# One quad more fetched row by row, from two queues, and the second last quad folded into one table

## The chip, the cores and the metric

The kernel runs on one core of a Trainium2 chip. Its engines are named as in the profile: PE (TensorE), DVE (VectorE), ACT (ScalarE), POOL (GpSimd) and SP (SyncE, which here only issues DMAs and loads registers). The metric is the device time of one execution in microseconds (us); the median of several runs is compared.

## The reference

A layer of graph attention. 12,500 nodes with 128 features, 200,000 edges sorted by their target `dst`, four heads of 32:

```python
h = relu(layernorm(x)) @ W_node.T                  # per node, 4 heads x 32
att = a . [h[src], h[dst], edge @ W_edge.T]        # per edge and head
att = where(att > 0, att, 0.2 * att)
m = maximum(segment_max(att, dst), 0)
ex = exp(att - m[dst])
denom = segment_sum(ex, dst) + (E - deg) * exp(-m)
out = x + segment_sum(ex / denom[dst] * h[src], dst)
```

## The kernel before

**Tiling.** The edges are cut into 392 groups of 511 edges and one entry that carries a running sum in. A group is 4 chunks of 128 edges, four groups are a *quad* (98 quads, 0 to 97), and one to four quads are a *super* whose softmax is done at once (the last supers have 2, 2 and 1 quads). A node's row in the DRAM tensor `table` has 137 floats (548 bytes): its 4 x 33 values, a count and 4 source logits.

**Rows by source.** The rows `h[src]` of a quad are 16 chunks of 128 rows. POOL fetches a chunk with one indirect DMA (`gather`, line 185), into one of eight places of `ga_all` (quad q into place q % 8). Quad 84 (`SINGLE`) is an exception: `gather` skips it, and SP fetches its 2,048 rows with one DMA each. `single_rows` (line 677) does eight rows at each step of `sums`, from quad 11 on: 16 steps a chunk, 256 steps, four steps a quad, so it ends with quad 74. Rows go into `GA[84]`, a part of `db_all` that is free after quad 9. The row numbers of a chunk are fetched by SP into one of two rows of 128 words (`fetch_places`), multiplied to byte offsets by DVE (`scale_places`) and loaded into registers 16 at a time (line 692). Two semaphores count the landings, and ACT waits for them in `add_sources` (line 790).

**Order of the work.** The program is written out by hand in Python generators that are stepped in turn; each engine works in the order in which its instructions are issued. In a stretch of the main loop (lines 1677 to 1711) `all_logits(q)` makes the attention logits of a quad with PE, DVE and ACT (it also asks for the gather of quad q + 2), `softmax(s)` does a super, and `sums(q)` weighs the gathered rows (`weighed`, line 1109), marks which edge goes to which node (`mark`) and adds up on PE (line 1186). `add_sources(q)` is where ACT copies the source logits out of the gathered rows (`U`, line 798): it waits there for the quad's gather. `all_logits(q)` calls it for quad q - 1 in the same stretch in which `sums(q - 5)` runs. `SP` loads features, offsets, weights and inputs two quads ahead (`issue`, line 606).

**Windows.** Quads 0 to 74 sum several groups into one window of nodes. From quad 75 on each group has a window of its own of 80 nodes: row 0 of its accumulator is the running sum of a node that goes on in the next group, so each window takes the row of the one before it in (`carried_in`, line 986, on ACT or DVE, then a matmul on line 983), and `copied_out` moves the accumulator to `pt`. A quad is then divided and its four windows are stored one by one (`divide`, `divide_by_gpsimd`); SP waits before each store to `out` until the one before it has landed.

**The end.** `finale` (line 1618) is the order of the last two supers, quads 95 and 96 and quad 97, written out. The last quad (`first_fold` = 97) is done by `folded` (line 1287): its four windows are moved into one table of 3 x 112 nodes by matmuls with 0/1 matrices (`SHIFT`, made by `shifts` on DVE four quads earlier), divided once and stored by one DMA (`finish`). Quad 96 goes through `sums` as others do, in two halves. `values_load` on line 1652 puts the flag that decides on the slow path (line 1714) into a register of every engine.

Of the kernel before, what the change touches and what calls it, by code (L numbers as in the profile page):

```python
# [14 lines left out]
OP = mybir.AluOpType  # L15
# [30 lines left out]
FOLDS, PARTS, FINE = 1, 3, 3  # L46
# [3 lines left out]
SINGLE, SINGLES_FROM, AT_A_STEP = 84, 11, 8  # L50
# [20 lines left out]
def kernel(  # L71
# [86 lines left out]
    first_fold = nq - FOLDS  # L158
    g_fold = quads[first_fold][0]
    assert class_of(first_fold) == (1, NARROW)  # L160
# [9 lines left out]
    single_came = [tc.alloc_semaphore(f"single{k}") for k in range(2)]  # L170
    landings = {}

    def gather(q, rows, width, lo, hi):

        if q == SINGLE:
            return
# [38 lines left out]
    assert [m for _, m in supers[-FINE:]] == [2, 2, FOLDS] and quads[-1][1] == QG  # L215
# [332 lines left out]
    with tc.tile_pool(name="work", bufs=2) as work, \  # L548
# [74 lines left out]
        def fetch_inputs(q):  # L623
# [3 lines left out]
            if q >= first_fold:  # L627
                at = ROWS[q] = windows(base_row, 4 * D, w, 1)
                due["inputs"].append((as_bytes(xw[1:1 + WIDE, 0:PARTS, :]), nodes_at(x, at[0])))
                return  # L630
# [12 lines left out]
        def fetch_rows(s):  # L643
            g0, m = groups(s)
            dr = DR[s] = turned.tile([SBG * H, NE + 2], I32, name="dr", bufs=2)
            if finer(s) > 1:
# [8 lines left out]
        n_own = QG * J * ROW  # L655
        GA[SINGLE] = own[:, QG * GE // 2:QG * GE // 2 + n_own].bitcast(F32).rearrange(
            "p (g j r) -> p g j r", g=QG, j=J)
        places = [own[0:1, QG * GE // 2 + n_own + k * P:QG * GE // 2 + n_own + (k + 1) * P]
                  for k in range(2)]
        single = {"step": 0, "landings": 0}  # L660
        steps = -(-P // AT_A_STEP)

        def fetch_places(n):

            if n >= QG * J:
                return
            g, j = quads[SINGLE][0] + n // J, n % J
# [3 lines left out]
        def scale_places(n):  # L671

            if n < QG * J:
# [3 lines left out]
        def single_rows():  # L677
# [5 lines left out]
            if n >= QG * J:  # L683
# [6 lines left out]
            lo = at * AT_A_STEP  # L690
            if at % 2 == 0:
                single["values"] = nc.values_load_multi_w_load_instructions(
                    places[n % 2][:, lo:lo + 2 * AT_A_STEP], engines=[mybir.EngineType.SP],
                    min_val=0, max_val=(NP - 1) * 4 * ROW,
                    skip_runtime_bounds_check_because="a node's row")[1]
            for p in range(lo, lo + AT_A_STEP):
                came = nc.sync.dma_start(
                    as_bytes(GA[SINGLE][p:p + 1, n // J, n % J, :]),
                    rows_at(table, single["values"][p - at // 2 * 2 * AT_A_STEP], 4 * ROW, 1))
                came.then_inc(single_came[2 * n // (QG * J)], 16)  # L700
# [1236 lines left out]
```

## Time and profile before

| | |
|---|---|
| median of 3 runs | 1971.07 us (1969.68 to 1973.94) |
| the profiled execution | 1973.07 us, span of its instructions 1971.2 us |
| busy: POOL, DVE, PE, PE weight load, ACT | 1477.5, 1193.8, 1134.6, 771.6, 318.1 us |
| mean granted TensorE clock | 0.739 |
| share of the DMA engines that the queues took: POOL's, SP's, ACT's | 24.5%, 21.0%, 0.4% |

A span is cut by time (windows), by instruction group (line, engine, operation), by wait (who waited for whom: total us, times, longest) or followed back from its last instruction (the chain). In a timeline a row is: start, duration, engine, line, operation, out<-in; the bracket holds the idle time before it and who ended that. "SPq" and "ACTq" are the queues of an engine that issue DMAs and load registers, not its arithmetic. In a view of one line, durations are in ns as minimum/median/maximum, then the first and the last start.

### The profile page before, as it was taken

How to read it: one execution, taken by the hardware profiler on the slowest of the kernel's cores; microseconds unless marked ns; L12 is line 12 of the kernel's file. 1: busy time of each engine (PE TensorE's matmuls, PEld its weight loads, DVE VectorE, ACT ScalarE, POOL GpSimd, SP SyncE). 2: the span in 40 equal slices, each digit the busy share in tenths (PEclk: the TensorE clock that was granted, in tenths of full speed). 3: DMA queues.
4: the chain of work that ended last, by engine and by line, in shares of the span. 5: the costliest groups of instructions: out<-in, count | busy, mean ns of one | idle time of the engine just before them, and what ended most of it. 6: DMA issues, size and time to landing. Idle time of an engine off the chain costs nothing.

```text
span 1971.2 us, 23138 instructions
## 1 busy us (share of the span) xinstructions
PE 1134.6 (58%) x5116; PEld 771.6 (39%) x5116; DVE 1193.8 (61%) x2631; ACT 318.1 (16%) x1077; POOL 1477.5 (75%) x1569
## 2 busy tenths in 40 slices
PE   6666676454555554646556555555464755555565
PEld 4544444333333342434334333344242433334344
DVE  8676887365464663746546546466374663767576
ACT  6664111001010010100000101001011011212122
POOL 7777777777777777777777777777777777777775
PEclk9788788676776766767767677777676766877678
DMA  7754754434444444444444444444444444544442
GB/s 257 209 134 100 177 135 107 106 93 107 103 106 107 102 113 102 117 101 118 104 119 103 114 108 113 110 112 110 113 109 99 105 122 109 128 114 116 98 107 56
DMA packets 171399, 229.87 MB, mean 117 GB/s; under 512 B 62636, under 2 KB 104542, under 8 KB 171255
## 3 DMA queue, kind: packets, MB, share of 16 engines
q0 software_dynamic: 49600, 108.49, 24.5%
q1 hardware_dynamic: 119952, 117.28, 21.0%
q10 hardware_dynamic: 1702, 2.59, 0.4%
q14 instruction: 104, 0.84, 0.1%
q8 instruction: 41, 0.67, 0.1%
HBM read 210.75 MB, written 17.43 MB: 116 GB/s over the span
## 4 chain that ended last, share of the span: by engine, by line
POOL 29%; DVE 27%; PE 15%; issue 13%; DMA 9%; ACT 5%; SPq 2%; ACTq 0%; POOLq 0%; DVEq 0%
POOL ga L185 29%; DMA ga<-table,srci 6%; PE acc L1186 6%; DVE at L717 4%; PE t_ps L855 2%; PE lg L747 2%; DVE ga L1112 2%; DVE t_ps L869 1%; DVE t_ps L868 1%; DVE t_ps L935 1%; DVE t_ps L932 1%; PE lg L750 1%; DVE pt L1019 1%; DVE hot L1095 1%; PE ex_ps L950 1%
## 5 line engine op out<-in xcount | busy, mean ns | idle before, releaser
L185 POOL DMA_INDIRECT ga<-table,srci x1478 | 1399.8, 947 | 451.8 <-issue 408.9
L1186 PE MATMUL acc<-ga,hot 128*113 128x137 f32 (+1 forms) x2904 | 536.3, 344 | 83.9 <-DVE hot L1095 43.4
L1186 PEld LDWEIGHTS acc<-ga,hot 128*113 128x113 f32 (+1 forms) x2904 | 476.5, 214 | 183.8 <-issue 78.9
L1019 DVE SCALAR_TENSOR_TENSOR pt<-pt,spare,acc 1x133 f32<-1x133 f32 x113 | 38.3, 339 | 484.4 <-ACT den_of L1013 483.0
L750 PE MATMUL lg<-at,pw 112*96 112x512 bf16 (+2 forms) x392 | 155.8, 434 | 266.6 <-DVE at L717 239.4
L717 DVE TENSOR_TENSOR at<-const_ps,db 112x1024 bf16<-112x1024 f32 (+1 forms) x176 | 212.9, 1211 | 43.4 <-DMA db<-offset 41.6
L747 PE MATMUL lg<-ea,by_pair 128*96 128x512 f32 (+1 forms) x392 | 229.5, 671 | 7.1 <-ACT tg L760 7.1
L1153 DVE TENSOR_TENSOR ga<-ga,ex_ps 128x1056 f32<-128x1056 f32 x145 | 179.7, 1240 | 0.0
L855 PE MATMUL t_ps<-ident,U 128*64 128x128 f32 (+2 forms) x210 | 46.4, 391 | 216.6 <-ACT U L798 216.6
L798 ACT COPY U<-ga 128x64 f32<-128x64 f32 x97 | 28.7, 297 | 786.7 <-DMA ga<-table,srci 786.7
L1155 DVE TENSOR_TENSOR hot<-const_ps,slot 128x896 f32<-128x896 f32 (+1 forms) x147 | 144.2, 981 | 0.0
L855 PEld LDWEIGHTS t_ps<-ident,U 128*64 128x64 f32 (+2 forms) x210 | 36.5, 198 | 242.8 <-ACT U L798 239.5
L950 PE MATMUL ex_ps<-ident,stack 128*128 128x128 f32 x105 | 28.5, 423 | 173.0 <-DVE stack L942 162.3
L750 PEld LDWEIGHTS <-pw 112*96 112x96 bf16 (+2 forms) x392 | 54.3, 139 | 103.3 <-issue 97.8
L1038 PEld LDWEIGHTS acc<-pt,spare 1*2 1x2 f32 x226 | 14.0, 86 | 204.2 <-issue 195.4
L950 PEld LDWEIGHTS ex_ps<-ident,stack 128*128 128x128 f32 x105 | 18.5, 214 | 186.9 <-ACT stack L940 186.9
L1112 DVE TENSOR_TENSOR ga<-ga,ex_ps 128x528 f32<-128x528 f32 x92 | 63.6, 693 | 37.3 <-ACT xs L956 37.2
L185 POOL DMA_INDIRECT ga<-in_x_dram,srci x72 | 68.5, 951 | 23.3 <-issue 18.9
L760 ACT COPY tg<-lg 96x512 f32<-96x512 f32 (+1 forms) x51 | 29.5, 579 | 297.4 <-PE lg L750 297.4
L776 PE MATMUL t_ps<-tg,of_head 96*64 96x512 f32 (+3 forms) x96 | 72.4, 848 | 0.0
L776 PEld LDWEIGHTS t_ps<-tg,of_head 96*64 96x64 f32 (+3 forms) x96 | 11.9, 171 | 146.0 <-issue 144.0
L747 PEld LDWEIGHTS lg<-ea,by_pair 128*96 128x96 f32 (+1 forms) x392 | 63.4, 187 | 13.2 <-ACT tg L760 8.6
(222 smaller groups left out, 1306.8 us busy)
## 6 DMA issues: line engine op xcount, KB each, us to landing
ea<-in_edge_t_dram SPq DMA_DIRECT2D x196, 256.0 KB
db<-table SPq DMA_DIRECT2D x2048, 0.5 KB
ga<-table,srci POOLq DMA_INDIRECT x1478, 3.7
db<-offset SPq DMA_DIRECT2D x53, 256.0 KB
db<-in_dst_dram SPq DMA_DIRECT2D x20, 320.0 KB
db<-offset SPq DMA_DIRECT2D x35, 160.0 KB
table<-row SPq DMA_DIRECT2D x9, 616.5 KB
xt<-in_x_dram SPq DMA_DIRECT2D x9, 576.0 KB
```

The source lines that it names most:

```text
L185: came = nc.gpsimd.indirect_dma_start(out=ga[:, i, j, 0:width], out_offset=None, in_=rows, in_offset=bass.IndirectOffsetOnAxis(ap=srci[:, ...
L717: nc.vector.tensor_tensor(AT[q][:span, i:i + n, :].rearrange("p g e -> p (g e)"), part_ps[:span].to_broadcast([span, n * GE]), DB[q][:span ...
L747: nc.tensor.matmul(lg, by_pair[:, begin:begin + n], ea[:, i // 2, :], start=half == 0 and i == 0, stop=False, skip_group_check=True)
L750: nc.tensor.matmul(lg, PW[q][:span, begin:begin + n], at[:span, i, :], start=False, stop=full and i == quads[q][1] - 1, skip_group_check=True)
L776: nc.tensor.matmul(TP[s][:groups(s)[1] * H], of_head[supers[s][1], p][:n], tg[:n], start=p == 0, stop=False, skip_group_check=True)
L855: nc.tensor.matmul(t_ps[:R, j * P:(j + 1) * P], u[:, j, :R], ident, start=False, stop=j == C - 1, skip_group_check=True)
L950: nc.tensor.transpose(turned_ps[:, j, :], stack[:, j * P:(j + 1) * P], ident)
L1019: nc.vector.scalar_tensor_tensor(to, row(w + at), passing[:, w + at:w + at + 1], own, op0=OP.mult, op1=OP.add)
L1112: engine.tensor_tensor(val, val, weight.unsqueeze(3).to_broadcast([P, J, H, HW]), op=OP.mult)
L1153: nc.vector.tensor_tensor(val, val, weight.unsqueeze(3).to_broadcast([P, TWO * J, H, HW]), op=OP.mult)
L1155: nc.vector.tensor_tensor(hot[:, i:i + TWO, :, 1:1 + span].rearrange("p g j c -> p (g j) c"), lane_ps[:, 0:span].unsqueeze(1).to_broadcast ...
L1186: nc.tensor.matmul(acc, hot[:, i, j, 0:1 + span], ga[:, i, j, :], start=new and j == J - 1 and not second, stop=k > 1 and i % k == k - 1 a ...
```

## The change

Two things, and a third that follows from them.

- **Singles.** Quads 48 and 84 are both fetched row by row. A step still issues eight rows on SP, and now eight more on ACT: two blocks of 16 row numbers, one for each engine. A chunk takes 8 steps instead of 16, so 32 chunks take the same 256 steps (quad 48 in quads 11 to 42, quad 84 in 43 to 74). Both use one place of 20 chunks: quad 48 has chunks 0 to 15, quad 84 has 4 to 19, and it starts with its last four, so that it writes over quad 48's from quad 51 on. Each quad has a semaphore for each engine.
- **Fold.** Quad 96 is folded too: it has a `SHIFT` (made in `sums(92)`), one load of inputs, one division and one store. Its sums are a generator, `folding`, with all four weighings on POOL.
- **Order at the end.** The flag is loaded some steps earlier; the last super's `factors` come after the first weighing in `folded`; quad 96 is divided there (`finish(*banks.pop("shares"))`) between the weighing of quad 97 and its matmuls.

```diff
-FOLDS, PARTS, FINE = 1, 3, 3
+FOLDS, LAST, PARTS, FINE = 2, 1, 3, 3
-SINGLE, SINGLES_FROM, AT_A_STEP = 84, 11, 8
+SINGLES, SINGLES_FROM, AT_A_STEP, BESIDE = (48, 84), 11, 8, 4
...
-    first_fold = nq - FOLDS
-    g_fold = quads[first_fold][0]
+    first_fold, fold_from = nq - LAST, nq - FOLDS
+    g_fold = quads[fold_from][0]
...
-        if q == SINGLE:
+        if q in SINGLES:
             return
...
-            if q >= first_fold:
+            if q >= fold_from:
                 at = ROWS[q] = windows(base_row, 4 * D, w, 1)
...
+        n_chunks = QG * J + BESIDE
+        begin, till = QG * GE // 2, QG * GE // 2 + n_chunks * ROW
+        own_rows = own[:, begin:till].bitcast(F32).rearrange("p (c r) -> p c r", r=ROW)
+        for q, lo in zip(SINGLES, (0, BESIDE)):
+            GA[q] = own_rows[:, lo:lo + QG * J, :].rearrange("p (g j) r -> p g j r", j=J)
...
+        singles = [(0, c, c) for c in range(QG * J)] + [
+            (1, c, BESIDE + c) for c in chain(range(QG * J - BESIDE, QG * J),
+                                              range(QG * J - BESIDE))]
-        steps = -(-P // AT_A_STEP)
+        steps = P // (2 * AT_A_STEP)
...
-            lo = at * AT_A_STEP
-            if at % 2 == 0:
-                single["values"] = nc.values_load_multi_w_load_instructions(
-                    places[n % 2][:, lo:lo + 2 * AT_A_STEP], engines=[mybir.EngineType.SP],
...
-            for p in range(lo, lo + AT_A_STEP):
-                came = nc.sync.dma_start(
...
+            for e, (engine, of) in enumerate(((nc.sync, mybir.EngineType.SP),
+                                              (nc.scalar, mybir.EngineType.Activation))):
+                lo = (at // 2 * 2 + e) * 2 * AT_A_STEP
+                if at % 2 == 0:
+                    single[e] = nc.values_load_multi_w_load_instructions(
+                        places[n % 2][:, lo:lo + 2 * AT_A_STEP], engines=[of], min_val=0,
...
+                for v in range(AT_A_STEP * (at % 2), AT_A_STEP * (at % 2 + 1)):
+                    came = engine.dma_start(as_bytes(own_rows[lo + v:lo + v + 1, to, :]),
+                                            rows_at(table, single[e][v], 4 * ROW, 1))
+                    came.then_inc(single_came[2 * k + e], 16)
...
-            if aside:
+            if s == len(supers) - 1:
+                state["factors"] = factors
+            elif aside:
                 factors()
...
-            parts = (2,) if first_fold - 2 <= q < first_fold else ()
+            parts = (2,) if q == first_fold - 2 else ()
...
-                if first_fold - 4 <= q < first_fold - 4 + FOLDS:
+                if fold_from <= q + 4 < nq:
                     shifts(q + 4, i)
...
+        def folding(q):
+            ga, hot = GA.pop(q), HOT.pop(q)
...
+            for i in range(m):
+                weighed(nc.gpsimd, ga, i, weights_of(q, i))
+                chunks(q, i, ga, hot)
+                if not i:
+                    complete()
+                if i == 1:
+                    carried_in(q, 0, ga, None)
+                    copied_out()
+                    entering(q, ga, hot)
+                    copied(q, 0)
+                if i:
+                    copied(q, i)
+                if i == m - 1:
+                    for k in range(m):
+                        fold(q, k)
+                yield
+            banks["shares"] = shares(q)
+            yield
...
+            for i in range(m):
+                if i == m - 1:
+                    weighed(nc.gpsimd, ga, i, weights_of(q, i))
+                else:
+                    weighed(nc.vector, ga, i, heads[:, :, :, i])
+                if not i:
+                    state.pop("factors")()
+            carried_in(q, 0, ga, fac)
+            assert not divisions and "to copy" not in state and not begun
+            finish(*banks.pop("shares"))
+            chunks(q, 0, ga, hot)
+            chunks(q, 1, ga, hot)
+            entering(q, ga, hot)
...
-            older = chain(sums(last - 2), sums(last - 1))
+            older = chain(sums(last - 2), folding(last - 1))
...
             step(turned_last, turned_last, older, turned_last, turned_last, older)
+            redo = nc.values_load(flag[0:1, 0:1], min_val=0, max_val=1)
             step(turned_last, older, older, turned_last)
             divide_by_gpsimd(*due_division())
             together(turned_last)
             topped()
-            redo = nc.values_load(flag[0:1, 0:1], min_val=0, max_val=1)
             together(older)
```

`chunks`, `entering`, `copied`, `fold`, `shares` and `finish` are the steps that `folded` had before, taken out of it.

202 lines of the change are left out of this document (94 added, 108 removed).

## The prediction

> **What bounds the kernel now.** I read the shares of the chain that ended last and the costliest groups first, then the waits, then windows of equal length, to see whether the bound changes along the way.
>
> ```profile
> POOL 29%; DVE 27%; PE 15%; issue 13%; DMA 9%; ACT 5%; SPq 2%; ACTq 0%; POOLq 0%; DVEq 0%
> L185 POOL DMA_INDIRECT ga<-table,srci x1478 | 1399.8, 947 | 451.8 <-issue 408.9
> POOL ga L185 <- issue: 427.8, 1403, 0.3
> ACT U L798 <- DMA ga<-table,srci: 786.7, 77, 19.8
> ...
> 1000.00:1100.00 100.00, 54.80 (x229) 35.96 (x227) 53.69 (x96) 8.05 (x29) 75.60 (x81) 0.69 0.45 110
> 1600.00:1700.00 100.00, 58.58 (x252) 40.11 (x253) 63.95 (x112) 19.51 (x83) 75.67 (x80) 0.71 0.46 113
> ...
> 1894.87 0.94 POOL ga L185
> 1895.82 0.30 issue
> 1896.12 0.95 POOL ga L185
> ```
>
> POOL is busy 75.6% of both windows (fifth busy column; the order is PE, PE loads, DVE, ACT, POOL), whatever the others do there. It waits for nothing but its own issue, never over 0.3 us at a time: no place in `ga_all` is ever late. So POOL runs as fast as it can all the way, one gather each 1896.12 - 1894.87 = 1.25 us, and a quad of 16 takes 20.0 us. The other side of this is ACT, which waits 786.7 us for gathered rows, once for most quads. DVE and PE are busy 54 to 64% of a window. The chain's 27% on DVE is work that fits between two gathers; the bound is POOL's count of gathers.
>
> What a quad without gathers is worth can be read at quad 84, which is one already:
>
> ```profile
> 1687.55 0.28 ACT L798 COPY U<-ga 128x64 f32<-128x64 f32 x1
> 1696.36 0.30 ACT L798 COPY U<-db 128x64 f32<-128x64 f32 x1
> 1708.00 0.30 ACT L798 COPY U<-ga 128x64 f32<-128x64 f32 x1 [2.82 <-DMA ga<-table,srci]
> ```
>
> Quads 83, 84 and 85 copy their source logits 8.8 and 11.6 us apart, not 20, and at 85 ACT already waits for rows again. POOL lost no time on quad 84, and the rest made up the quad's work within one quad.
>
> **The change part by part.** *Gathers.* 16 fewer: 16 x 1.25 = **20.0 us** off POOL's queue, and all later rows come that much earlier. Nothing else on POOL changes before the end.
>
> *Who has to keep up.* While ACT takes quad Q's logits, `sums(Q - 4)` runs; with eight places POOL may then gather quads Q + 1 to Q + 3 before a place is missing. So the other engines may fall 60 us behind POOL before it stops. Quad 48 uses up 20 of them at once. The gain stays whole if, from quad 11 to 74, a quad costs SP and ACT less than 20.0 us, or so little more that the lag stays under 60.
>
> ```profile
> L697 SPq MOVE db<-table x2048: 29/29/38, 327.7 to 1601.6; - x187
> L697 SPq DMA_DIRECT2D db<-table x2048: 224/228/469, 327.8 to 1601.7; - x187
> L692 SPq TENSOR_LOAD <-db x128: 971/1167/1210, 326.5 to 1593.6; - x128
> L669 SPq DMA_DIRECT2D db<-in_src_dram x16: 223/269/275, 312.9 to 1437.2; - x16
> ...
> 1303.14 2.52 SPq L697 DMA_DIRECT2D db<-table  x8
> ...
> 1226.50 0.32 SPq L606 DMA_DIRECT2D pw<-side  x1
> 1245.36 0.32 SPq L606 DMA_DIRECT2D pw<-side  x1
> ```
>
> SP is the one that is nearly full. Eight rows take it 2.52 us, 0.315 each (0.228 and 0.029 of it are rows of the profile), and where it runs without much waiting one quad's round takes 1245.36 - 1226.50 = 18.86 us. It keeps its eight rows a step, its 16-value loads and its 256 steps. New are 16 more fetches of row numbers at 0.27 us over 64 quads, 0.07 us a quad: 18.93 of 20.0. After quad 48, SP can win back some 1 us a quad, and from quad 75 on, without singles, nearly everything at once, as at quad 84. Lag 20 us of 60, cost nothing.
>
> ACT gets what it has not done in the trace of before: 32 rows and two 16-value loads a quad. Lower bound, SP's prices: 32 x 0.315 + 2 x 1.17 = 12.4 us. Upper bound, from ACT's own issues:
>
> ```profile
> 0.76 0.41 ACTq L264 DMA_DIRECT2D wn<-in_w_node_dram  x1
> 0.76 0.42 SPq L222 DMA_DIRECT2D srci<-in_src_by_edge_dram  x1
> 1.20 0.45 ACTq L266 DMA_DIRECT2D we<-in_w_edge_dram  x1
> 1.23 1.40 SPq L462 DMA_DIRECT2D xt<-in_x_dram  x3
> ...
> L462 SPq DMA_DIRECT2D xt<-in_x_dram x13: 328/432/538, 1.2 to 55.3; - x13
> ...
> L1559 ACTq DMA_DIRECT2D rows<-in_dst_ends_dram x1: 245/245/245, 426.8 to 426.8; - x1
> L1652 ACTq TENSOR_LOAD <-flag x1: 487/487/487, 1955.2 to 1955.2; - x1
> ```
>
> At 0.45 an issue and the same gap of 0.087, 32 x 0.54 = 17.2, with loads 0.2 us dearer than SP's, 19.9 us. The nearest row is L1559, also from one partition: 0.245 on ACT against 0.269 on SP (L669). I take SP's price and 0.2 more a load: 12.8 us. ACT's own work is 8.05 us in 100, 1.6 a quad, so it has some 5 us a quad left for waiting on PE and DVE. Its bursts delay a softmax or a copy by 2 to 4 us; that is lag, and lag is covered by the 60 us. If the cover were gone, every us of lag would be a us of the end.
>
> *Waits added.* ACT waits at quad 48 for two semaphores whose last rows were issued six quads before: nothing. SP may fetch the next row numbers only when ACT has loaded those of two chunks before, so SP gets at most two steps ahead of ACT; queued behind it are singles, weights, features and offsets, for which DVE's line 717 waits two quads later. I take 0 to 2 us a super, and it can only bring SP to ACT's pace. Quad 84's rows go over quad 48's three quads after those were summed: nothing. DVE's 16 more scalings and one quad's shift matrices lie in windows where it is idle over a third.
>
> *The end.* Here the chain is compute again.
>
> ```profile
> 1929.12 0.30 ACT L798 COPY U<-ga 128x64 f32<-128x64 f32 x1 [5.00 <-DMA ga<-table,srci]
> ...
> 1954.33 0.30 PE L950 MATMUL ex_ps<-ident,stack 128*128 128x128 f32 x1 [1.42 <-ACT stack L940]
> 1955.23 1.93 DVE L1112 TENSOR_TENSOR ga<-ga,ex_ps 128x528 f32<-128x528 f32 x3
> 1963.94 0.56 DVE L1353 TENSOR_TENSOR res<-res,inputs 113x384 f32<-113x384 f32 x1
> ...
> 1960.96 1.42 PE t_ps L1327 x12
> ...
> 1962.52 0.32 SPq L606 DMA_DIRECT2D out_dram<-res  x1
> 1966.47 0.33 SPq L606 DMA_DIRECT2D out_dram<-res  x1
> SPq L606 <- DMA out_dram<-res: 22.5, 20, 1.8
> ...
> L1652 DVEq TENSOR_LOAD <-flag x1: 540/540/540, 1954.5 to 1954.5; - x1
> ```
>
> At quad 96 (1929.12) ACT still waits 5 us for rows, so the whole end moves up with the gathers. The last result is ready at 1963.94 + 0.56 = 1964.50, but its store is issued at 1966.47: SP first has to see the stores of quad 96 land, one after the other (20 such waits, 22.5 us). With four of them made one and issued some 4 us before, the **1.97 us** go. What is late next is the result itself. Folding quad 96 puts 1 + 2 + 3 + 3 shifts (18 matmuls) on PE, at 1.42 / 12 = 0.118 us each 2.1 us, ahead of the transposes of line 950; PE idles 1.42 us before these, so they come some 0.7 us later. In return `factors` and the flag's load (0.54 us on DVE) leave the place between those transposes and the weighing of 1955.23; but the load then stands earlier in the same DVE series, so I count only `factors`' share. Net the result is 0.4 to 0.9 later; I take 0.7. Gain at the end **1.3 us**, bounds -0.5 (folds and load wholly in the path) to 2.5.
>
> Sum: 20.0 + 1.3 = **21.3 us**. Span 1971.2 - 21.3 = 1949.9; with the 1.87 around it (1973.07 - 1971.2) 1951.8. The median of the runs shown, 1971.07, is 2.0 under that execution, so the forecast for the median is 1971.07 - 21.3 = **1949.8**.
>
> **The rivals.** *SP and ACT hold each other up at issuing (slower).* Were only one of them able to issue at a time, a burst of eight on one would meet a burst on the other, and each of SP's rows would wait the 0.228 of ACT's less the 0.087 between two of its own: 32 x 0.141 = 4.5 us a quad. SP would need 18.93 + 4.5 = 23.4; in 64 quads it falls 64 x 3.4 = 220 behind, 240 with quad 48, and POOL stops for all over 60: 1949.8 + 180 = 2130. The gain shrinks from 1.7 us a quad on, and from 2.0 a quad the kernel is slower than before. Against it: at 0.76 and 1.20 both queues issue at once, and SP's took 0.42 and, three in 1.40, 0.44 each, where the median of that line, mostly alone, is 0.432. That is 0.01 a row at most, 0.3 us a quad. Chance 0.14. [...]
>
> *ACT's queue is the slow one (part of the gain).* With the upper price, 19.9 + 1.6 and a us of waiting, a quad costs ACT 22.5: 64 x 2.5 + 20 - 60 = 120 us late. Between the prices lies the point from which it counts: 20.6 a quad, a row of 0.45. Just above it the kernel gives back part of the 20: 1953 to 1971. Against it is row L1559. Chance 0.10, half of it within 0.2% of before.
>
> *The end gives its part back.* Folds and flag load both in the path, the last store no earlier: 1971.07 - 20.0 + 2 = 1953. Chance 0.09.
>
> *The change doesn't free POOL:* a gather of another quad would have to take longer. The 75.6% of POOL is the same with SP's singles (1000 to 1100) and after them (from 1602). Left out.
>
> **How the numbers follow.** Forecast 1949.8, chance 0.66 with the end's bounds and the spread of the runs (1947 to 1952.5); the end's rival 0.09; ACT's 0.10; the hold-up 0.14, and 0.01 between. The range reaches from 1946.5 over the first two and the near part of ACT's to 1961. About 0.2%, 4 us, can be told from no change: faster 0.66 + 0.09 + 0.05 = 0.80, within 0.06, slower 0.14.
>
> **What would show it.** Right: 1462 gathers at 1.25 us, POOL waiting only for issue, its last gather some 20 us earlier; ACT's rows near 0.23 us and SP's L697 rows unchanged; ACT without a wait for rows for some quads after 48, and with one again at quads 90 to 96; the last store right behind the last result. Wrong: SP's rows over 0.28 us (hold-up), POOL waiting for a matmul or for DVE between quads 30 and 80 (lag over 60), or a last result over a us later behind the gathers than now.

## The result and the profile after

The changed kernel takes **1952.8 us** (median of 4 runs, 1952.21 to 1953.43) against 1970.77 us (1969.68 to 1973.94) for the kernel before beside it: a ratio of 0.9905, 95% interval 0.9893 to 0.9918. The forecast was 1949.8, the range 1946.5 to 1961.0. The profiled execution took 1952.87 us with a span of 1951.1, so the two profiled executions are 20.2 us apart, the two medians 18.0.

One thing has to be known to read what follows: in five of the six groups of experiments the kernel before itself took 2631 to 2650 us, with SP's instructions standing still for 0.7 us at a time, so every run is compared only with the kernel before of its own group.

The answers to the rows shown of before come from the page (the shares of the chain, the group of gathers) and from the waits, and then from two windows (PE, PE loads, DVE, ACT and POOL busy, granted clock, DMA share, GB/s).

```profile
DVE 24%; POOL 18%; issue 13%; PE 11%; SPq 10%; DMA 8%; ACTq 8%; ACT 4%; DVEq 0%; POOLq 0%
...
L185 POOL DMA_INDIRECT ga<-table,srci x1462 | 1384.2, 947 | 446.9 <-issue 412.4
```

```profile
ACT U L806 <- DMA ga<-table,srci: 436.6, 49, 16.5
POOL ga L185 <- issue: 431.6, 1415, 0.3
...
DVE at L724 <- DMA db<-offset: 218.9, 35, 11.7
```

```profile
1000.00:1100.00 100.00, 61.40 (x266) 40.24 (x264) 59.12 (x108) 9.93 (x33) 75.56 (x81) 0.76 0.45 111
1600.00:1700.00 100.00, 58.37 (x289) 39.57 (x287) 64.30 (x102) 20.17 (x87) 75.83 (x80) 0.81 0.51 130
```

There are 16 gathers fewer, and POOL is as busy as before, 75.6 to 75.8% of a window; from 300 us on it still never waits over 0.3 us between two gathers, nearly always for its own issue. ACT waits for rows 49 times instead of 77. DVE now waits 218.9 us for offsets: SP is later with them, though not late enough for POOL to notice. The chain shows SP's and ACT's queues at 18% together, where they had 2%; POOL's count of gathers is the bound all the same, for POOL has no longer wait, and the last gather starts 20.7 us earlier (1923.28, below, against 1943.96; how far such a difference of two single executions can be trusted is said with the experiments).

The rows of the singles, from the view of their line (ns minimum/median/maximum, first and last start):

```profile
L705 SPq DMA_DIRECT2D db<-table x2048: 224/228/358, 327.3 to 1593.0; - x187
...
L705 ACTq DMA_DIRECT2D db<-table x2048: 227/235/547, 327.4 to 1575.9; - x187
```

SP's rows are what they were, 0.228 us, and 64 quads' worth of them takes (1593.0 - 327.3) / 64 = 19.8 us a quad, POOL's pace; before it was (1601.7 - 327.8) / 64 = 19.9. ACT's rows take 0.235.

The copies of the source logits around quad 48 (ACT's timeline; quad 48 is the copy from `db`):

```profile
972.52 0.30 ACT L806 COPY U<-ga 128x64 f32<-128x64 f32 x1 [6.41 <-issue]
...
987.07 0.30 ACT L806 COPY U<-db 128x64 f32<-128x64 f32 x1
...
1067.23 0.30 ACT L806 COPY U<-ga 128x64 f32<-128x64 f32 x1 [9.39 <-DMA ga<-table,srci]
```

From quad 48 to quad 52 no copy waits for rows; at quad 53 (1067.23) ACT has caught up and waits 9.39 us for POOL again.

### The profile page after: what moved, and what is told of

The parts are those of the page before. It is cut to its first block, busy times and chain, and to the rows that moved or that the text cites. A ratio compares the mean times of both kernels' runs of the same rounds, so it can differ in the third digit from the quotient of the medians.

```text
span 1951.1 us, 27435 instructions
## 1 busy us (share of the span) xinstructions
PE 1136.9 (58%) x5134; PEld 769.5 (39%) x5134; DVE 1202.5 (62%) x2658; ACT 323.7 (17%) x1073; POOL 1461.8 (75%) x1553
## 3 DMA queue, kind: packets, MB, share of 16 engines
q14 instruction: 136, 1.11, 0.2%
## 4 chain that ended last, share of the span: by engine, by line
DVE 24%; POOL 18%; issue 13%; PE 11%; SPq 10%; DMA 8%; ACTq 8%; ACT 4%; DVEq 0%; POOLq 0%
POOL ga L185 18%; ACTq L705 7%; SPq L705 6%; PE acc L1196 4%; DMA ga<-table,srci 4%; DVE at L724 3%; DMA db<-offset 3%; SPq L606 2%; DVE ga L1163 2%; PE lg L754 2%; DVE t_ps L943 1%; DVE t_ps L877 1%; DVE t_ps L876 1%; DVE t_ps L940 1%; DVE ga L1122 1%
## 5 line engine op out<-in xcount | busy, mean ns | idle before, releaser
L185 POOL DMA_INDIRECT ga<-table,srci x1462 | 1384.2, 947 | 446.9 <-issue 412.4
L1196 PE MATMUL acc<-ga,hot 128*113 128x137 f32 (+1 forms) x2848 | 514.9, 339 | 83.7 <-DVE hot L1105 52.2
L1196 PEld LDWEIGHTS acc<-ga,hot 128*113 128x113 f32 (+1 forms) x2848 | 457.1, 210 | 179.4 <-issue 89.8
L724 DVE TENSOR_TENSOR at<-const_ps,db 112x1024 bf16<-112x1024 f32 (+1 forms) x176 | 213.3, 1213 | 219.0 <-DMA db<-offset 218.9
L754 PE MATMUL lg<-ea,by_pair 128*96 128x512 f32 (+1 forms) x392 | 254.9, 738 | 95.3 <-ACT tg L767 95.3
L757 PE MATMUL lg<-at,pw 112*96 112x512 bf16 (+2 forms) x392 | 160.0, 447 | 176.0 <-DVE at L724 161.0
L1163 DVE TENSOR_TENSOR ga<-ga,ex_ps 128x1056 f32<-128x1056 f32 x143 | 177.4, 1240 | 0.0
L754 PEld LDWEIGHTS lg<-ea,by_pair 128*96 128x96 f32 (+1 forms) x392 | 68.7, 203 | 105.3 <-ACT tg L767 100.6
L958 PEld LDWEIGHTS ex_ps<-ident,stack 128*128 128x128 f32 x105 | 18.5, 214 | 194.6 <-ACT stack L948 194.6
L783 PE MATMUL t_ps<-tg,of_head 96*64 96x512 f32 (+3 forms) x96 | 60.9, 720 | 45.0 <-ACT tg L767 45.0
L1094 ACT CAST hot<-is_last 128x16 f32<-128x16 bf16 x98 | 21.1, 217 | 188.9 <-issue 185.1
```

The lines of the kernel that those rows point to most:

```text
L185: came = nc.gpsimd.indirect_dma_start(out=ga[:, i, j, 0:width], out_offset=None, in_=rows, in_offset=bass.IndirectOffsetOnAxis(ap=srci[:, ...
L724: nc.vector.tensor_tensor(AT[q][:span, i:i + n, :].rearrange("p g e -> p (g e)"), part_ps[:span].to_broadcast([span, n * GE]), DB[q][:span ...
L754: nc.tensor.matmul(lg, by_pair[:, begin:begin + n], ea[:, i // 2, :], start=half == 0 and i == 0, stop=False, skip_group_check=True)
L757: nc.tensor.matmul(lg, PW[q][:span, begin:begin + n], at[:span, i, :], start=False, stop=full and i == quads[q][1] - 1, skip_group_check=True)
L783: nc.tensor.matmul(TP[s][:groups(s)[1] * H], of_head[supers[s][1], p][:n], tg[:n], start=p == 0, stop=False, skip_group_check=True)
L958: nc.tensor.transpose(turned_ps[:, j, :], stack[:, j * P:(j + 1) * P], ident)
```

## Where the end went

The tail behind the last gather is 27.80 us (1951.08 - 1923.28); before it was 27.24 (1971.20 - 1943.96). Instead of a gain of 1.3 us there is a loss of 0.6. The timeline of the changed kernel's end:

```profile
1923.28 0.94 POOL L185 DMA_INDIRECT ga<-table,srci  x1 [0.30 <-issue]
...
1927.63 0.29 ACT L806 COPY U<-ga 128x64 f32<-128x64 f32 x1
...
1935.60 0.27 PE L958 MATMUL ex_ps<-ident,stack 128*128 128x128 f32 x1
...
1936.27 0.70 DVE L1122 TENSOR_TENSOR ga<-ga,ex_ps 128x528 f32<-128x528 f32 x1 [1.10 <-ACT xs L964]
1936.61 1.09 POOL L1122 TENSOR_TENSOR ga<-ga,xe 128x528 f32<-128x528 f32 x1
1936.89 0.82 DVE L934 TENSOR_TENSOR fac<-ends 1x4 f32<-1x4 f32 x1
1937.75 0.15 DVE L935 TENSOR_TENSOR fac<-ends,fac 1x4 f32<-1x4 f32 x1
1937.83 1.30 DVE L1122 TENSOR_TENSOR ga<-ga,ex_ps 128x528 f32<-128x528 f32 x2
...
1945.58 0.56 DVE L1351 TENSOR_TENSOR res<-res,inputs 113x384 f32<-113x384 f32 x1
1946.17 0.33 SPq L606 DMA_DIRECT2D out_dram<-res  x1
```

The last store is issued at 1946.17, right behind the last result (1945.58 + 0.56): the wait of 1.97 us is gone, as forecast. But the result is 22.9 us behind the last gather, where it was 20.5. The series of three weighings on DVE, 1.93 us before, lasts from 1936.27 to 1939.13, 2.86 us: `factors` stands inside it, and the first of its two operations on four elements took 0.82 us while POOL weighed the last group, the second 0.15. In its old place, ahead of the weighings, it was little cheaper: 0.13 us and, beside another operation of POOL, 0.59 (rows in the last section). But there it ran, with the flag's load, while DVE had to wait for the transposes anyway: the first weighing started 0.24 us behind ACT's copy of the transposes (`xs`, done at 1954.99, weighing at 1955.23), and it starts 0.03 us behind it now (1936.24 and 1936.27). So the moves saved 0.2 us just ahead of the weighings, and `factors` cost 0.9 inside them.

Part of this is probably not the change's. Just ahead, in the 5.3 us behind the copy of quad 96, PE's granted clock was 0.50 and not 0.68 (windows of the changed kernel, then of the kernel before; the clock is the first figure behind the five busy times):

```profile
1908.70:1914.00 5.30, 5.22 (x15) 3.05 (x16) 3.51 (x10) 0.72 (x4) 4.08 (x5) 0.50 0.50 134
```

```profile
1929.40:1934.70 5.30, 5.23 (x18) 2.87 (x19) 3.98 (x14) 0.71 (x4) 4.08 (x5) 0.68 0.39 92
```

PE had stood idle just ahead of it for the same time, 3.84 us in the changed kernel and 3.87 in the kernel before. The last copy of source logits comes 4.35 us behind the last gather, where it came 3.35. Which part of that is the clock's, the first pair of experiments below shows, as it has the old end at a clock of 0.50.

## The experiments

**One part alone, twice.** The first kernel is the kernel before with the singles of the change and its own end; the second is the kernel before with the new end and its own singles.

```diff
 FOLDS, PARTS, FINE = 1, 3, 3
-SINGLE, SINGLES_FROM, AT_A_STEP = 84, 11, 8
+SINGLES, SINGLES_FROM, AT_A_STEP, BESIDE = (48, 84), 11, 8, 4
```

```diff
-FOLDS, PARTS, FINE = 1, 3, 3
+FOLDS, LAST, PARTS, FINE = 2, 1, 3, 3
 SINGLE, SINGLES_FROM, AT_A_STEP = 84, 11, 8
```

> Only the single rows of quads 48 and 84, issued by SyncE and ScalarE; the end of the kernel as before (one quad folded). Theory A (the whole gain is POOL's 16 gathers of 1.25 us, the end gives nothing): 20.0 us less than before, 1534 gathers, POOL waiting for issue alone, the tail behind the last gather's start 27.2 us as before. Rival B (the single rows cost something elsewhere and the fold makes up for it): less than 19 us gained, with the last gather less than 19 us earlier. Rival C (the fold costs 1.9 us against the prediction's end): 21 us or more gained.

> Only the end: the second last quad shifted into one table, divided and stored once; singles as before (quad 84 by SyncE alone), 1550 gathers. The prediction's step: 1.3 us less than before. What the two traces show: the wait of 1.97 us for the store goes, but the last result comes 2.3 us later behind the last gather instead of 0.7, so the tail is 0.6 us longer: before plus 0.6 us. Rival (1.0 us of those 2.3 is TensorE's granted clock of 0.50 for some 5 us in that one execution, and not the change): before less 0.4 us, with that stage at a clock of 0.64 to 0.70.

> The same kernel as in the first experiment (single rows of quads 48 and 84 by SyncE and ScalarE, end as before), run once more because there the kernel before itself took 2650 us instead of 1971, with SyncE's rows standing still for 0.70 us at a time. If the kernel before takes 1971 us here, theory A (only the 16 gathers count): 20.0 us less than before, last gather 20 to 20.7 us earlier, rows of SyncE at 0.228 us and no stops. If the stops are there again: as in the first experiment, some 7% slower than before.

> The same kernel as in the second experiment (only the new end), once more for the same reason. Where the kernel before takes 1971 us: the prediction's step gives 1.3 us less than before; the traces' reading 0.6 us more; the rival, that 1.0 us of it is the granted clock of one execution, 0.4 us less. If SyncE's rows stop again, SyncE is the bound, the end counts little, and it is within 0.3% of before as it was.

| | this, us | before, us | ratio, 95% interval |
|---|---|---|---|
| e1_singles | 2834.24 | 2650.34 | 1.0688 (1.0654 to 1.0723) |
| e2_fold | 2656.04 | 2650.34 | 0.9997 (0.9967 to 1.0027) |
| e5_singles_again | 1954.09 | 1972.1 | 0.9904 (0.9887 to 0.992) |
| e6_fold_again | 1971.5 | 1972.1 | 0.9996 (0.9987 to 1.0006) |

(The ratio is worked out from the single executions and is not quite the quotient of the two medians.)

Where the kernel before takes 1972 us, the singles alone give the gain (18.9 us by the ratio, 15.8 to 22.3) and the new end nothing that can be told from zero (0.8 us, -1.2 to 2.6): the median can't choose between the three values expected of it, and the tails below have to. Theory A's 20.0 lies in its interval. One part of what was expected of e5 did not come: its last gather starts at 1926.71, 17.2 us before that of the kernel before and not 20 to 20.7. By these two figures rival B, a cost elsewhere, would fit too. POOL's waits speak against it: in e5, too, none between two gathers is over 0.3 us from 300 us on. What differs is the pitch of the gathers in one execution: from the first start to the last it is (1926.71 - 93.83) / 1461 = 1.2545 us in e5, 1.2525 in the changed kernel with the same gathers, 1.2528 in the kernel before and 1.2517 in e6. Over 1,461 gathers that makes up to 4 us, so neither 17.2 nor the 20.7 of the first pair is better known than that; e5's profiled execution is also 2.6 us over its median. Why the pitch differs was not followed.

Where the kernel before takes 2650 us, the same singles make the kernel 6.9% slower. That was not expected by any theory of the first kernel, and is taken up below.

The tails of the two runs at 1972 us, with those of before and after, each worked out from rows like these two timelines' (the old end of e5, the new end of e6):

```profile
1926.71 0.94 POOL L185 DMA_INDIRECT ga<-table,srci  x1 [0.30 <-issue]
...
1930.69 0.29 ACT L806 COPY U<-ga 128x64 f32<-128x64 f32 x1
...
1938.61 1.93 DVE L1120 TENSOR_TENSOR ga<-ga,ex_ps 128x528 f32<-128x528 f32 x3
...
1947.29 0.56 DVE L1361 TENSOR_TENSOR res<-res,inputs 113x384 f32<-113x384 f32 x1
```

```profile
1942.40 0.94 POOL L185 DMA_INDIRECT ga<-table,srci  x1 [0.31 <-issue]
...
1946.73 0.30 ACT L798 COPY U<-ga 128x64 f32<-128x64 f32 x1
...
1955.38 0.70 DVE L1114 TENSOR_TENSOR ga<-ga,ex_ps 128x528 f32<-128x528 f32 x1 [1.10 <-ACT xs L956]
...
1966.23 0.56 DVE L1343 TENSOR_TENSOR res<-res,inputs 113x384 f32<-113x384 f32 x1
```

| us | before (old end) | e5 (old end) | changed (new end) | e6 (new end) |
|---|---|---|---|---|
| last gather to last copy of logits | 3.35 | 3.98 | 4.35 | 4.33 |
| to the first weighing | 7.92 | 7.92 | 8.64 | 8.65 |
| to the result | 9.27 | 9.24 | 9.87 | 11.41 |
| to the end of the span | 6.70 | 7.05 | 4.96 | 4.47 |
| tail | 27.24 | 28.17 | 27.80 | 28.86 |

e5 has the clock of 0.50 of the changed kernel and the old end: 0.6 of the first row goes with the clock, and the new end against the old one is 27.80 - 28.17 = **0.4 us gained**, not 1.3. (That is one pair of executions; the old end alone differs by 0.35 in the last row between the kernel before and e5.) The last row gives 2.1 us, about the 1.97 forecast; the three above it give back 0.4 + 0.7 + 0.6 = 1.7, where 0.7 were forecast. What the 0.4 ahead of the last copy come from was not followed further. The 0.7 can be taken apart in the timelines: DVE stands still for 0.42 us at the flag's load (1930.89 to 1931.31 in the changed kernel, nothing before); PE's transposes start 0.65 us behind the end of ACT's `stack` and not 0.12 (1934.95 to 1935.60 against 1954.21 to 1954.33), as the folds are in the way; and the 0.2 that `factors` and the load held up the weighings are gone. The 1.5 us more in e6's third row go with the clock again: it is 0.50 there from 1958.2 to 1960.2 and 0.80 for two more, and 1.00 in the changed kernel at the same place.

```profile
1958.20:1960.20 2.00, 2.00 (x10) 2.00 (x10) 1.65 (x7) 0.15 (x1) 0.00 (x0) 0.50 0.06 12
```

```profile
1939.10:1941.10 2.00, 2.00 (x19) 1.92 (x18) 1.65 (x7) 0.69 (x4) 0.00 (x0) 1.00 0.05 10
```

**SP alone, and more work on ACT.** The changed kernel with all 16 rows of a step on SP; and the changed kernel with 16 copies more on ACT at each step.

```diff
-            for e, (engine, of) in enumerate(((nc.sync, mybir.EngineType.SP),
-                                              (nc.scalar, mybir.EngineType.Activation))):
+            for e, (engine, of) in enumerate(((nc.sync, mybir.EngineType.SP),
+                                              (nc.sync, mybir.EngineType.SP))):
```

```diff
+        idle = consts.tile([P, 64], F32, name="idle")
...
                     single["landings"][k] += 16
+            for _ in range(16):
+                nc.scalar.copy(idle, idle)
```

> The changed kernel with ScalarE's eight rows and its load of 16 row numbers given to SyncE as well, so that SyncE issues 16 rows a step. Lag theory: SyncE needs 18.9 + 12.4 = 31.3 us a quad where POOL needs 20.0; the others fall 11.3 us a quad behind, POOL stops when that passes 60 us, about five quads after the singles begin, and in 64 quads the loss is 64 x 11.3 + 20 - 60 = 683 us: about 2640 us. Rival (SyncE's queue holds up only quad 48's own rows, other transfers are early enough): under 2100 us.

> The changed kernel with 16 copies of 128 x 64 from a tile into itself on ScalarE behind each step of single rows, 64 a quad; at a pitch of 0.15 to 0.16 us that is 10 us a quad. ScalarE's own 14.6 us a quad (32 rows 10.5, two loads 2.5, its work 1.6) become 24.8. Lag theory: 4.8 us a quad too much, 64 x 4.8 + 20 - 60 = 267 us: about 2220 us, more by what ScalarE waits for other engines inside a quad. Rival 1 (ScalarE waits in a chain, every us on it is a us of the quad): 64 x 10 - 60 = 580: 2530 us. Rival 2 (ScalarE is nowhere near the bound): 1953 us.

> The same kernel as e4_act_16 (16 more copies of 128 x 64 on ScalarE behind each step of single rows), once more because the chip of that run stopped SyncE's rows. Where the kernel before takes 1971 us: the lag theory gives 24.8 us a quad on ScalarE, 64 x 4.8 + 20 - 60 = 267 us more than the changed kernel, about 2220 us, more by what ScalarE waits inside a quad; POOL waits for a place from about quad 20 on. Rival 1 (every us on ScalarE is a us of the quad): 2530 us. Rival 2 (ScalarE is far from the bound): 1953 us.

All three ran where the kernel before took 2632 to 2650 us: e3 3424.85 us (ratio 1.2922, 1.2855 to 1.2988), e4 3064.77 (1.1563, 1.1506 to 1.1621), e10 3036.28 (1.1534, 1.1458 to 1.161). So the 60 us of allowed lag were not tested against POOL's pace and stay open; the totals expected don't apply. What they do give is the price of rows. The view of the singles' line in e2 (32 rows a quad on SP, none on ACT), e1 (32 and 32) and e3 (64 on SP):

```profile
L697 SPq DMA_DIRECT2D db<-table x2048: 1/228/1420, 488.8 to 2229.0; - x187
```

```profile
L705 SPq DMA_DIRECT2D db<-table x2048: 1/228/1411, 495.0 to 2401.8; - x187
...
L705 ACTq DMA_DIRECT2D db<-table x2048: 2/235/1399, 495.1 to 2378.2; - x187
```

```profile
L705 SPq DMA_DIRECT2D db<-table x4096: 1/228/1408, 493.3 to 3003.0; - x196
```

Over 64 quads that is 27.2, 29.8 and 39.2 us a quad: SP, not POOL, sets the pace, and 32 rows and two loads more on SP cost 39.2 - 27.2 = 12.0 us, where the prediction's price is 12.4. The pace explains the times: e3 is (39.2 - 29.8) x 64 = 602 us over e1 by it, and 591 by the medians. The median row is still 0.228 us; what is new are rows of 1 ns and of 1.4 us, bunches and stops. SP's timeline in e1 shows eight rows taking 12.79 or 8.59 us, and between them 3.12:

```profile
1203.21 12.79 SPq L705 DMA_DIRECT2D db<-table  x8
...
1217.70 3.12 SPq L705 DMA_DIRECT2D db<-table  x8
...
1222.29 8.59 SPq L705 DMA_DIRECT2D db<-table  x8
```

In the changed kernel at 1952.8 us nearly every eight take 2.5 to 2.6 us (1130.20 2.56, 1133.85 2.51, 1138.74 2.57 in its timeline).

On ACT the copies had a pitch of 4.38 / 16 = 0.27 us (a row of e10's ACT timeline) and not the 0.16 assumed, which is what lies between a copy of the source logits, 128 x 64 as well, and ACT's next operation in the changed kernel (1131.24 and 1131.40), so 17.5 us a quad were added, not 10; and ACT's rows run over (2589.5 - 476.8) / 64 = 33.0 us a quad.

```profile
1505.00 4.38 ACT L714 COPY idle<-idle 128x64 f32<-128x64 f32 x16 [3.97 <-issue]
```

```profile
L707 ACTq DMA_DIRECT2D db<-table x2048: 3/235/1397, 476.8 to 2589.5; - x187
```

Without the copies ACT's own work is then at most 33.0 - 17.5 = 15.5 us a quad; the prediction has 12.8 + 1.6 = 14.4. So ACT has room in the 20 us of a quad, about what was forecast.

**The end in another order.** The changed kernel with `factors` ahead of the weighings again, the folds of quad 96 behind the transposes of the last super, and the flag's load behind them.

```diff
-            if s == len(supers) - 1:
-                state["factors"] = factors
-            elif aside:
+            if aside:
                 factors()
...
-                if i == m - 1:
-                    for k in range(m):
-                        fold(q, k)
                 yield
+            for k in range(m):
+                fold(q, k)
             banks["shares"] = shares(q)
...
-            redo = nc.values_load(flag[0:1, 0:1], min_val=0, max_val=1)
             step(turned_last, older, older, turned_last)
             divide_by_gpsimd(*due_division())
             together(turned_last)
             topped()
+            redo = nc.values_load(flag[0:1, 0:1], min_val=0, max_val=1)
             together(older)
```

> The changed kernel with its end in another order: the folds of quad 96 behind the transposes of the last super, the factors again ahead of the last weighing, and the flag's load again behind the transposes. My reading of the tails (new end against old end at the same granted clock): of 1.7 us that the last result comes later, 0.4 is the flag's load, 0.5 the folds ahead of the transposes, 0.9 the factors between the weighings. If that is right, the last result is ready 21.1 to 21.4 us behind the last gather's start instead of 22.9, the span ends 26.2 us behind it instead of 27.8, and the median is 1.6 us under the changed kernel's 1952.8, some 20.5 us under before. Rival (the late result comes from TensorE's granted clock, not from the order): 22.9 and 27.8 as in the changed kernel.

It took 2801.14 us beside 2631.58 (1.0636, 1.0594 to 1.0678), so the median says nothing of the end. The stretch from the last copy of logits to the result can still be compared, with e1 (old end) and e2 (new end). The timeline of e7, then of e2:

```profile
2778.90 0.29 ACT L806 COPY U<-ga 128x64 f32<-128x64 f32 x1
...
2786.82 1.94 DVE L1120 TENSOR_TENSOR ga<-ga,ex_ps 128x528 f32<-128x528 f32 x3
...
2796.24 0.56 DVE L1349 TENSOR_TENSOR res<-res,inputs 113x384 f32<-113x384 f32 x1
```

```profile
2633.66 0.29 ACT L798 COPY U<-ga 128x64 f32<-128x64 f32 x1
...
2642.31 0.70 DVE L1114 TENSOR_TENSOR ga<-ga,ex_ps 128x528 f32<-128x528 f32 x1 [1.09 <-ACT xs L956]
...
2651.62 0.56 DVE L1343 TENSOR_TENSOR res<-res,inputs 113x384 f32<-113x384 f32 x1
```

From the copy to the first weighing e7 needs 7.92 us, as the old end does, and e2 8.65; the weighings take 1.94 us again. So those three moves together were what made the weighings late. (Seen from the last gather, which starts at 2709.1, 70 us ahead of the copy, the end says nothing here, as POOL is not what it waits for.) But the result comes 17.9 us behind the copy, against 18.5 in e2 and 17.2 in e1: of the 1.6 us won, 1.0 is lost again behind the weighings, where the folds of quad 96 now stand on PE ahead of the last quad's sums. That they are the cause was not shown apart. Half of the reading was right: the order costs the time, but the folds have to go somewhere.

**Four more chunks.** That kernel with the first group of quad 93 fetched singly as well, in sums 75 to 82, in the places of quad 48's first group.

```diff
-SINGLES, SINGLES_FROM, AT_A_STEP, BESIDE = (48, 84), 11, 8, 4
+SINGLES, SINGLES_FROM, AT_A_STEP, BESIDE, PART = (48, 84), 11, 8, 4, 93
...
         ga = GA[q] = ga_all[:, q % QUADS]
+        if q == PART:
+            GA[q] = Parted(own_rows[:, 0:J, :], ga)
+            lo = max(lo, 1)
...
                                               range(QG * J - BESIDE))] + [
+            (2, c, c) for c in range(J)]
```

> The kernel with that end, and four more chunks of 128 rows fetched singly: the first group of quad 93, in the places of quad 48's first group, by SyncE and ScalarE in sums 75 to 82. Lag theory: 4 gathers of 1.25 us less, 5.0 us more gained, as SyncE and ScalarE still keep within 60 us of POOL (20 for quad 48, 20 for quad 84, 5 here): 1946 us, 25 us under before, POOL waiting for issue alone. Rival (they are at their limit and need quads 75 to 82 to catch up): POOL waits for a place between quads 84 and 92, and the gain over the other end alone is under 3 us.

> The same kernel as e9_best (the end in the other order, four more chunks fetched singly), once more because there the kernel before took 2632 us and SyncE, not POOL, set the pace. Where the kernel before takes 1971 us: the lag theory gives 5.0 us for the four gathers and about 1 us for the end (measured there: 0.6 us less from the last copy of source logits to the result), so 1946 to 1947 us, a ratio of 0.988, POOL waiting for issue alone, last gather 25 us before that of the kernel before. Rival (SyncE and ScalarE need quads 75 to 82 to catch up): POOL waits for a place between quads 84 and 93 and the gain over the changed kernel is under 3 us. Where SyncE's rows stop again: 8% slower than before, as there.

> The same kernel as e9_best, once more. Where the kernel before takes 1971 us: 1946 to 1947 us (5.0 us for four gathers and about 1 us for the end under the changed kernel), POOL waiting for issue alone, the last gather 25 us before that of the kernel before, the result 17.9 us behind the last copy of source logits instead of 18.5. Rival: POOL waits for a place between quads 84 and 93 and the gain over the changed kernel is under 3 us. Where SyncE's rows stop again: 8% slower than before, as in the two runs before.

Three times it ran where the kernel before took 2632 to 2633 us: 2856.9 us (1.0835, 1.0787 to 1.0884), 2862.54 (1.0862, 1.0816 to 1.0909), 2844.21 (1.0823, 1.0784 to 1.0861). The size of that is again SP's pace: 256 steps of e7 cost (2374.3 - 494.4) / 64 = 29.4 us a quad; behind them e7 needs 2802.0 - 2374.3 = 427.7 us and e9 2856.4 - 2611.4 = 245.0 with eight quads fewer to go, 22.8 us for a quad without singles. Eight quads at 29.4 instead of 22.8 make 53 us, and e9 is 56 over e7. The end was expected to need 17.9 us from the last copy to the result, as in e7; it needed 18.3 in e9 and in e13, and 19.9 in e11, where the granted clock fell to 0.55 on the way (2866 to 2868). So e7's order of the end is worth 0.3 to 0.6 us against the 18.5 of the changed kernel. Whether the four chunks would give their 5 us where POOL sets the pace was not measured.

```profile
L705 SPq DMA_DIRECT2D db<-table x2048: 2/228/1415, 494.4 to 2374.3; - x187
```

```profile
L719 SPq DMA_DIRECT2D db<-table x2304: 1/228/1408, 492.8 to 2611.4; - x192
```

**No single rows at all.** The changed kernel with quads 48 and 84 gathered by POOL.

```diff
-SINGLES, SINGLES_FROM, AT_A_STEP, BESIDE = (48, 84), 11, 8, 4
+SINGLES, SINGLES_FROM, AT_A_STEP, BESIDE = (), 999, 8, 4
```

> The changed kernel without any single rows: quads 48 and 84 are gathered by POOL too, 32 more gathers. Theory where the kernel before takes 1971 us: 16 more gathers than before at 1.25 us, 20.0 us more than before (1991 us), 40 more than the changed kernel; SyncE 12 us a quad freer, which gains nothing. Theory where the kernel before takes 2630 to 2650 us: there SyncE's single rows alone set the pace of 27 us a quad, so without them POOL's 20 us a quad is the bound again and the kernel takes about 1991 us, a quarter less than before. Rival there (all of SyncE's transfers are slow, or POOL is held up too): still over 2300 us.

2413.64 us beside 2631.17 (0.9159, 0.909 to 0.9229); three of its four executions took 2411 to 2415 us, one took 3100, and why that one did is not known. The rival of this experiment holds: single rows are about a third of the loss there (the kernel before is 660 us over its 1971), but without them the kernel is still 420 us over POOL's 1991. SP then has time left (it waits 321.6 us for results to store), yet its other instructions also stand still for 0.7 us at times (a DMA at 1407.76 takes 0.70, where one of the same kind takes 0.34 at 1416.42); what sets the pace of this kernel was not followed. There it is the fastest of all that ran; at POOL's pace it would, by the estimate, lose the 20 us a quad that single rows give, so no version was found that beats both kernels in both conditions. The row from SP's waits:

```profile
SPq L606 <- DVE res L1438: 321.6, 36, 23.2
```

## Why the prediction was right or wrong

- **The bound, and 20.0 us for 16 gathers: right as far as can be measured.** POOL waits for nothing else, and e5 gets the gain from the singles alone, 18.9 us with 20.0 inside the interval. That the last gather of the profiled pair starts 20.7 us earlier is partly luck: e5's starts 17.2 earlier, with the pitch of one execution as the difference.
- **Who has to keep up: right where POOL sets the pace.** SP's rows at 0.228 us, ACT's at 0.235 (forecast near 0.23), SP at POOL's pace. Where SP stops, the price of 32 rows and two loads was 12.0 us on SP (12.4 by the prediction) and ACT's own work at most 15.5 us a quad (14.4). The 60 us of cover were never used up at POOL's pace and stay untested. A slip in the rival on ACT's queue changes nothing: of its 20.6 us a quad, 1.6 of own work, a us of waiting and two loads of 1.37 leave 15.3 for 32 rows, which is a row of 0.39 and not of 0.45. One remark was wrong: SP was to win back 1 us a quad after quad 48, and everything only from quad 75. In fact ACT waits for rows again at quad 53; what SP is late with is needed late, so SP's lag is not ACT's.
- **The end: wrong, by 1.9 us of tail.** The step that failed is "Net the result is 0.4 to 0.9 later; I take 0.7". At equal clock it is 1.7 later. The folds ahead of the transposes came out about as counted, 0.5 us for the 0.7: PE ran from the folds straight into the transposes (no idle time in front of 1935.60, where the kernel before had 1.42). The flag's load and `factors` were counted as no cost and as a gain; the load sits in DVE's series ahead of the transposes and costs 0.4 there; that both left their old place gains 0.2, but `factors` makes the weighings 0.9 longer, as it stands between two of them while POOL weighs beside it. 0.4 ahead of the last copy are unexplained. The 1.97 us of the store are right. Some 0.6 more of the tail goes with the clock.
- **From the profile to the median: 2.0 us.** The gain was worked out in one profiled execution of the kernel before, which stood 2.0 us over its median; the changed kernel's stands 0.07 over its own. So 20.2 us between the two profiled executions are 18.0 between the medians. As a sum, 1.9 of the tail, less the 0.7 by which the last gather came earlier than forecast, and 1.9 of these offsets give the 3.0 between 1949.8 and 1952.8 to within 0.1. Only the tail's part has a cause that was looked into; the other two are differences of single executions.
- **The rival "The end gives its part back": its number, half of its mechanism.** The measured 1952.8 lies 0.3 us outside the 1947 to 1952.5 of the main case and 0.2 from this rival's 1953. Folds and flag's load are in the path, as it says, at 0.5 and 0.4 us; but the store is not late, and the 0.9 of `factors` are not in it. That the totals agree is luck.
- **The rival "SP and ACT hold each other up": not here, but elsewhere.** At 1952.8 us nothing of it shows: in the trace of the changed kernel the 1,208 rows of SP that overlap a row of ACT take 235 ns on average, the other 840 take 234. Where the kernel before takes 2650 us, ACT's rows beside SP's go with 29.8 - 27.2 = 2.6 us a quad more on SP (2.2 in e7), and since SP is the bound there, the change loses: 2.6 x 64 = 166 of the 178 us between e1 and e2. SP doesn't spend them waiting for ACT or another engine: all its waits in the stretch of the single rows add up to 16 us in e1 and 11 in e2. Whether ACT's rows cause the longer stops was not shown apart from these pairs. The price given was 4.5, and "slower from 2.0 a quad" was the right kind of threshold, though for another reason: there SP has no slack at all, even alone. ACT's rows alone are not what the stops rest on: in e2, where ACT issues none, a row of SP takes up to 1.42 us too, and at 1952.8 us, with both queues issuing, none takes over 0.36 on SP or 0.55 on ACT.

## What to carry to other kernels

Work moved off the bounding engine was worth its count times its pitch here, 16 x 1.25 us against 18.9 measured with the singles alone, where the engines that took it over kept up; but such a gain rests on their slack, and where that slack is gone (SP at 27 us a quad instead of 19.9) the same change loses 7%. A tiny instruction put between two long ones on the critical engine is better priced by what it takes in that place than by its duration elsewhere: the first of `factors` took 0.82 us there, beside an operation of POOL, and 0.15 in the median. And a difference between two profiled ends can go with the clock of one execution, here 0.6 and 1.5 us: compare the parts at equal granted clock first.

## What the runs showed of the hardware

- **Queues that stop.** In those five groups of runs, the instructions of SP (and those of ACT where it issues rows) came in bunches a few ns long and in steps of about 0.70 us or twice that (rows of 1 ns and of 1.4 us above; SP's DMAs for `inputs` in e1 take 0.71 and 0.70 us at 1220.84 and 1232.28), and the kernel before took 2631 to 2650 us. PE, DVE and POOL show no such steps in e1's timeline from 1200 to 1240 us: a gather takes 0.94 to 1.11 us there, DVE's weighing (L1161) 1.24 and eight matmuls (1204.33 and 1207.78) 1.19; in the changed kernel these are 0.94 to 0.95, 1.24 to 1.25 and, at 1140.95, 1.19. It is not a property of one chip: the record gives the same chip for the pair e5 and e6, at 1972 us, and for e13, at 2633. What causes it stays open; it was not tried apart.
- **The clock of one execution.** The stretch behind the copy of quad 96 ran at a granted clock of 0.68 in the execution of the kernel before and at 0.50 in those of the changed kernel, e5 and e6, behind the same idle time of PE (3.84 to 3.88 us in before, after and e6); a second place, in e6, ran at 0.50 and in the changed kernel at 1.00. The end is 0.6 and 1.5 us longer with the lower clock. As e5 and e6 have no part of the change in common, I take it for a matter of the single execution and not of the change; that is an estimate, as the kernel before was not profiled twice to show it, and what sets the clock was not shown.
- **Four elements at 0.82 us.** The two operations of `factors` take 0.15 us each in the median of their 28 times. In the changed kernel's end the first took 0.82, where POOL's weighing of 1.09 us begins 0.28 us ahead of it and ends with it (1937.70 and 1937.71), and the second, behind that, 0.15. In the kernel before the second took 0.59 beside an operation of POOL that ends with it (1955.10 and 1955.11), and the first, ahead of that, 0.13. The longest of the 28 is 0.59 in e1, e5, e7, e9 and e13, with `factors` in the old place, and 0.82 in e2, e6 and e12, with it in the new one; in all ten traces it ends 12 to 19 ns behind an operation of POOL. In the old place the flag's load on DVE's queue covers the same time (1954.53 to 1955.07 in the kernel before), so there the two can't be told apart; in the new place there is no load. DVE's three weighings in the kernel before (1955.23 to 1957.16) were not held up beside POOL's (1955.87 to 1956.96): 0.64 us each, and 0.65 for the two that ran without it in the changed kernel.

```profile
1954.35 0.13 DVE L926 TENSOR_TENSOR fac<-ends 1x4 f32<-1x4 f32 x1
...
1954.49 0.61 POOL L1418 TENSOR_TENSOR res<-pt,others 81x256 f32<-81x256 f32 x1 [2.94 <-DVE fac L926]
1954.52 0.59 DVE L927 TENSOR_TENSOR fac<-ends,fac 1x4 f32<-1x4 f32 x1
```
